# A scan that starts at a constant: where the carried state of a selective scan enters, and who copies it

## The chip, the core and the metric

The kernel runs on one core of a Trainium2 chip. The core has five engines that work at the same time, each through its own queue in the order written: PE (TensorE, matrix products and transposes), DVE (VectorE), ACT (ScalarE), POOL (GpSimd) and SP (SyncE, which here issues nearly all DMAs). An engine that reaches an instruction whose inputs are not there stands still, with all that is queued behind it. The metric is the device time of one execution in microseconds (us), as a median over several runs.

## The reference

The input x is 8 sequences of 2048 rows with 512 channels. The computation is a selective-scan (Mamba) layer followed by a quantised linear layer, both with a residual. Cut to what matters:

```
u     = layernorm(x)
xp    = u @ x_proj_w.T                      # 64 ranks, 16 B, 16 C per row
delta = softplus(xp[:64] @ dt_proj_w.T + b) # per row and channel
for each state n of 16, each channel d, along the rows t:
    h[t] = exp(delta[t,d] * A[d,n]) * h[t-1] + delta[t,d] * B[t,n] * u[t,d]     (h before the first row is 0)
    y[t,d] += h[t] * C[t,n]
x = x + y + u * D
z = layernorm(x);  q = round(z / scale) as int8, scale = max|z| / 127 per row
out = x + (q @ wq.T) * scale * w_scale + bias
```

## The kernel before

The rows are cut into 32 chunks of T = 512 rows; four chunks make one sequence (`CPB` = 4). Channels lie on the 128 partitions in ND = 4 blocks d. Within a chunk the 16 states n follow each other, and within a state the four blocks, which gives `SLOTS` = 64 slots per chunk. The main loop (L972 to L1004) goes through all slots u, with s = u // 4 the running number of the state and d = u % 4. For each slot it emits, in this order: `c_mult` of the state before and every second state a `load_c` (at d = 0), some exponentials, a piece of B for two states later, the matmuls `b_pe` for slot u + 2, the scan of slot u, the transposes `y_pe` for a state some 11 slots back, and whatever the table of planned steps has for this slot. All engines receive their instructions in this order; nothing is reordered later.

What each part does:

- `exp_unit` (L706): ACT computes da = exp(delta * A) for one state and block, 128x512. It runs ahead of the scans by a lead that the tuples `EXP_NONE` (no exponential in this slot) and `EXP_TWO` (two) shape; the lead starts at 7. Ten buffers of 128x512 hold the results.
- `bt_piece` (L715) and `b_pe` (L733): the input term delta*B*u. For ten of the states ACT scales a tile by B (L728) and PE transposes it (L751); for the six `DIAG_STATES` a diagonal matrix comes by DMA (L723) and PE multiplies with it (L742). The result stays in one of three PSUM buffers.
- `scan` (L754): DVE runs the recurrence over 512 rows of one block with one instruction. Its initial value is `0.0 if k % CPB == 0 else state[n][:, d : d + 1]`: a constant in the first chunk of a sequence, and in the other three a column per partition, the state carried from the chunk before. Below, these are called constant chunks (8 of them) and state chunks (24).
- `c_mult` (L779): POOL first copies the last column of h, four numbers per partition, into `state[n]` (L785, not in the last chunk of a sequence), and then multiplies h, 128x2048, with C (L788). h and its product hc have three buffers each.
- `load_c` (L770): SP loads two states' C rows at a time, broadcast over the partitions, into one of three buffers.
- `y_pe`: PE transposes hc and sums it up in PSUM.

Around this, the layer norm, projections and softplus of the next chunk (`prep`) and the residual, quantisation and output of the previous chunk (`post`) are spread over the slots by the tables `PREP_AT` and `POST_AT`; a number is the slot in the chunk that the entry is planned against, and `LATE_AT` takes the place of `POST_AT` near the end. Steps named below: `aggregate` (DVE, L240) finishes the row statistics; `rstd` (POOL, L246 to L252) makes 1/sqrt of them, four small instructions; `norm` of `post` (ACT, L589) applies it; `amax` (DVE, L608) takes the row maxima; `scales` (POOL, L615) writes xs from them; `inverses` (DVE, L620) takes its reciprocal; `dt_pe` (PE, L344) and `softplus` (ACT, L354) make delta through a single PSUM buffer, so that they alternate; `add_bias` (POOL, L601) and `add_x1` (POOL, L669) add 128x1024 tiles. In one slot the steps of `post` stand ahead of those of `prep`.

Of the kernel before, what the change touches and what calls it, by code (L numbers as in the profile page):

```python
# [9 lines left out]
F32 = mybir.dt.float32  # L10
# [17 lines left out]


PREP_AT = dict(  # L30
    stats=(-54, -53, -52, -50),
    aggregate=(-50, -48, -46, -45),
    rstd=-37,
    norm=(6, 6, 7, 10),
    xnt_pe=(10, 12, 13, 15),
    xnt_act=(12, 13, 15, 17),
    xp_pe=(17, 18, 21, 21),
    xp_act=24,
    bt_pe=26,
    bt_act=26,  # L40
    dt_pe=(27, 30, 31, 32),
    softplus=(27, 30, 32, 34),
    dlt_pe=(36, 38, 40, 42),
    du=(37, 39, 41, 43),
)

POST_AT = dict(
    load=(-10, 3),
    residual=(10, 13, 14, 14),
    stats=(15, 17, 19, 23),  # L50
    aggregate=(19, 22, 22, 24),
    rstd=27,
    norm=(29, 29, 29, 34),
    amax=(31, 36),
    scales=37,
    inverses=41,
    add_bias=(30, 38),
    rnd=(47, 47, 49, 49),
    q_pe=(48, 53, 59, 65),
    q_act=(51, 55, 60, 66),  # L60
    o_pe=(57, 62, 68, 71),
    o_out=(59, 64, 70, 73),
    add_x1=(65, 75),
    store=(75, 79),
    add_x=(-1, 0, 8, 10),
)
# [21 lines left out]

Y_BEHIND = 11

LAST_LOAD = (30, 56)
LAST_ADD_X = (50, 52, 61, 62)
SKIP_AT = (44, 46, 55, 57)
EXP_NONE = (6, 8, 9, 11, 12, 16, 18, 20, 28, 29, 30, 31, 32, 33, 34, 37, 45, 50, 51, 54, 56, 62)
EXP_TWO = (0, 1, 3, 4, 10, 15, 19, 22, 23, 24, 35, 36, 39, 41, 42, 43, 46, 53, 57, 58, 61, 63)


@with_exitstack
def kernel(
# [20 lines left out]
    ND = DM // P  # L120
# [4 lines left out]
    CPB = L // T  # L125
# [6 lines left out]
    const = ctx.enter_context(tc.tile_pool(name="const", bufs=1))  # L132
    xpool = ctx.enter_context(tc.tile_pool(name="xp", bufs=3))
    chan = ctx.enter_context(tc.tile_pool(name="chan", bufs=2))
    bcp = ctx.enter_context(tc.tile_pool(name="bc", bufs=3))
    work = ctx.enter_context(tc.tile_pool(name="work", bufs=2))
    small = ctx.enter_context(tc.tile_pool(name="small", bufs=6))
    dram = ctx.enter_context(tc.tile_pool(name="dram", bufs=2, space=bass.MemoryType.DRAM))
    diagd = ctx.enter_context(tc.tile_pool(name="diagd", bufs=1, space=bass.MemoryType.DRAM))
    ps_y = ctx.enter_context(tc.tile_pool(name="ps_y", bufs=1, space=bass.MemoryType.PSUM))  # L140
# [3 lines left out]
    pin = tc.keep_in_program_order  # L144
# [19 lines left out]
    alog_sb = const.tile([P, ND, N], F32, name="alog_sb")  # L164
# [21 lines left out]
    pin(nc.vector.memset(zeros, 0.0))  # L186


    a_exp = const.tile([P, ND, N], F32, name="a_exp")
    pin(nc.scalar.activation(a_exp, alog_sb, AF.Exp))  # L190
    a_neg = const.tile([P, ND, N], F32, name="a_neg")
    diag_d = const.tile([P, ND, P], F32, name="diag_d")
# [80 lines left out]
    def prep(k):  # L273
# [120 lines left out]
    def prep_first(second):  # L394
# [113 lines left out]
        bc = dram.tile([N, T], F32, tag="bc", name="bc_0")  # L508
# [9 lines left out]
        )  # L518
        dt(2)
        dt(3)  # L520
        load_c(0)
        for s in range(2):
            bts[s] = work.tile([P, NT, P], F32, tag="dg", bufs=2, name=f"dg_0_{s}")
            for i in range(NT):
# [5 lines left out]
        for d in range(ND):  # L530
# [8 lines left out]
            t = x[:, :, ts(d, P)]  # L539
# [164 lines left out]
    LAST = NCHUNK * N  # L704

    def exp_unit(u):  # L706
        s, d = divmod(u, ND)
        if s >= LAST:
            return
        k, n = divmod(s, N)  # L710
        t = work.tile([P, T], F32, tag="da", bufs=10, name=f"da_{k}_{n}_{d}")
        pin(nc.scalar.activation(t, delta[k][:, d, :], AF.Exp, scale=a_neg[:, d, n : n + 1]))  # L712
        das[u] = t

    def bt_piece(s, i):  # L715

# [37 lines left out]
    def scan(u):  # L754
        s, d = divmod(u, ND)
        k, n = divmod(s, N)
        if d == 0:
            hs[s] = work.tile([P, ND, T], F32, tag="h", bufs=3, name=f"h_{k}_{n}")
        pin(
            nc.vector.tensor_tensor_scan(  # L760
                hs[s][:, d, :],
                das.pop(u),
                pbs.pop(u),
                0.0 if k % CPB == 0 else state[n][:, d : d + 1],
                ALU.mult,
                ALU.add,
            )
        )

    def load_c(s):  # L770

        if s >= LAST:
            return
        k, n = divmod(s, N)
        t = bcp.tile([P, 2, T], F32, tag="c", name=f"c_{k}_{n}")
        pin(nc.sync.dma_start(out=t, in_=bcs[k][ds(n, 2), :].partition_broadcast(P)))
        cts[s // 2] = t

    def c_mult(s):  # L779
        if s < 0 or s >= LAST - 1:  # L780
            return
        k, n = divmod(s, N)
        h = hs.pop(s)
        if k % CPB != CPB - 1:
            pin(nc.gpsimd.tensor_copy(state[n], h[:, :, T - 1]))  # L785
        hc = work.tile([P, ND, T], F32, tag="hc", bufs=3, name=f"hc_{k}_{n}")
        c = cts[s // 2][:, n % 2, :]
        pin(nc.gpsimd.tensor_tensor(hc, h, c.unsqueeze(1).to_broadcast([P, ND, T]), ALU.mult))  # L788
        hcs[s] = hc
# [51 lines left out]
    def finish():  # L841


        k, s = NCHUNK - 1, LAST - 1
        h = hs.pop(s)
        hc = work.tile([P, ND, T], F32, tag="hc", bufs=3, name=f"hc_{k}_{N - 1}")
        c = cts[s // 2][:, (N - 1) % 2, :]
# [115 lines left out]
    ahead = 7  # L963
    for u in range(ahead):
        exp_unit(u)
    for k in range(NCHUNK):
        plan(k * SLOTS, [(SKIP_AT[i], lambda k=k, i=i: skip_pe(k, i)) for i in range(NT)])
        if k < NCHUNK - 1:
            plan((k + 1) * SLOTS, post(k))
        if k + 1 < NCHUNK:  # L970
            plan(k * SLOTS, [at for at in prep_of[k + 1] if at[0] >= 0 or k > 0])
    for u in range(NCHUNK * SLOTS + Y_BEHIND):  # L972
        k, slot = divmod(u, SLOTS)
        s, d = divmod(u, ND)
# [79 lines left out]
```

## Time and profile before

| what | us |
|---|---|
| median of 3 runs | 2894.75 |
| the runs | 2892.88 to 2896.7 |
| the profiled execution, its own time | 2885.92 |
| its span, first to last instruction | 2884.0 |

| engine | busy us | share |
|---|---|---|
| DVE | 2805.6 | 97% |
| PE | 2766.2 | 96% |
| POOL | 2759.9 | 96% |
| ACT | 2691.9 | 93% |

How to read it: "busy" counts the time in which at least one instruction of the engine was under way. Successive instructions of an engine overlap by some tens of nanoseconds, so the cost of one in a dense row is the distance between two starts, which is less than its duration. The ends of matmuls are modelled, so PE can show as busy while it could take more. A row of instruction groups gives the line, the engine, the operation, out<-in with shapes and the count, then busy time and the mean duration in ns, then the idle time ahead of these instructions and what ended it. A row of the timeline gives start and duration in us, then the same, and in brackets a wait. The granted TensorE clock was 0.992 of full speed over the execution.

### The profile page before, as it was taken

What the parts mean: (1) busy time and instruction counts of PE and PEld (TensorE: products, weight loads), DVE (VectorE), ACT (ScalarE), POOL (GpSimd) and SP (SyncE); (2) the same over time, 40 slices, a digit from 0 to 9 for tenths busy, and PEclk for the clock granted to TensorE, in tenths of its full rate; (3) what the DMA queues carried; (4) which work ended last, traced back from release to release, by engine and by line L of the source; (5) the groups of instructions that cost most, each with busy time, mean ns of one, the idle gap of its engine ahead of it and who ended that gap; (6) DMA issues with size and microseconds to landing.
All of it is one profiled execution on the core that took longest, in us unless ns stands there. A gap on an engine that the chain in (4) does not pass through costs nothing.

```text
span 2884.0 us, 79269 instructions
## 1 busy us (share of the span) xinstructions
PE 2766.2 (96%) x32978; PEld 2350.9 (82%) x32978; DVE 2805.6 (97%) x2949; ACT 2691.9 (93%) x4350; POOL 2759.9 (96%) x1219
## 2 busy tenths in 40 slices
PE   8999999999999999999999999999999999999997
PEld 7888888888888888888888888888888888888875
DVE  6999999999999999999999999999999999999996
ACT  7999999999999999999999999999999999999985
POOL 6899999999999999999999999999999999999997
PEclk9999999999999999999999999999999999999998
DMA  4333333433333333333333333334333333433331
GB/s 149 107 94 89 110 106 111 108 93 97 108 102 117 95 91 106 110 111 104 97 93 111 101 118 96 91 101 115 111 104 95 95 112 100 118 86 101 87 112 51
DMA packets 223655, 295.80 MB, mean 103 GB/s; under 512 B 114048, under 2 KB 114560, under 8 KB 223296
## 3 DMA queue, kind: packets, MB, share of 16 engines
q1 hardware_dynamic: 222240, 290.51, 34.9%
q8 instruction: 258, 4.23, 0.6%
q14 instruction: 101, 0.83, 0.1%
q10 hardware_dynamic: 1056, 0.23, 0.0%
HBM read 252.55 MB, written 38.14 MB: 101 GB/s over the span
## 4 chain that ended last, share of the span: by engine, by line
PE 56%; DVE 26%; issue 8%; ACT 8%; DMA 2%; SPq 0%; POOL 0%; DVEq 0%; ACTq 0%
DVE h L760 20%; PE pb L751 13%; PE pb L742 13%; PE y L810 13%; ACT da L712 3%; PE pdt L344 3%; PE y L831 3%; PE pxp L305 3%; PE po L648 3%; ACT bT L728 2%; PE y L556 2%; PE pz L631 2%; DVE st L236 2%; DVE x L367 2%; DVE am L608 1%
## 5 line engine op out<-in xcount | busy, mean ns | idle before, releaser
L788 POOL TENSOR_TENSOR hc<-h,c 128x2048 f32<-128x2048 f32 x511 | 2327.3, 4560 | 25.4 <-DVE h L760 11.2
L760 DVE TENSOR_TENSOR_SCAN h<-da,state,pb 128x512 f32<-128x512 f32 x1536 | 1859.2, 1260 | 19.2 <-PE pb L742 13.7
L712 ACT ACTIVATE da<-delta,a_neg 128x512 f32<-128x512 f32 x2048 | 1382.6, 714 | 43.4 <-DVE h L760 38.4
L728 ACT ACTIVATE bT<-x,BT 128x512 f32<-128x512 f32 x1276 | 893.7, 713 | 0.0
L742 PE MATMUL pb<-dg,x 128*128 128x128 f32 x6176 | 811.2, 280 | 14.1 <-DMA dg<-dg 8.7
L742 PEld LDWEIGHTS pb<-dg,x 128*128 128x128 f32 x6176 | 746.6, 192 | 76.2 <-DVE h L760 37.7
L751 PE MATMUL pb<-ident,bT 128*128 128x128 f32 x5104 | 731.9, 277 | 47.2 <-DVE h L760 22.0
L751 PEld LDWEIGHTS pb<-ident,bT 128*128 128x128 f32 x5104 | 576.6, 141 | 205.9 <-DVE h L760 77.9
L760 DVE TENSOR_TENSOR_SCAN h<-da,pb 128x512 f32<-128x512 f32 x512 | 591.0, 1200 | 26.6 <-PE pb L742 8.3
L810 PE MATMUL y<-ident,hc 64*128 64x64 f32 x16384 | 613.2, 225 | 0.2
L810 PEld LDWEIGHTS y<-ident,hc 64*128 64x128 f32 x16384 | 547.5, 139 | 73.4 <-issue 48.4
L236 DVE BATCH_NORM_STATS2 st<-x 128x6 f32<-128x512 f32 x244 | 162.9, 668 | 0.0
L669 POOL TENSOR_TENSOR z<-z,x 128x1024 f32<-128x1024 f32 x62 | 149.6, 2412 | 0.0
L601 POOL TENSOR_TENSOR x<-x,bias_b 128x1024 f32<-128x1024 f32 x62 | 146.8, 2368 | 2.5
L344 PE MATMUL pdt<-xp,dtproj_sb 128*128 128x512 f32 x248 | 136.4, 632 | 10.6 <-ACT delta L354 10.2
L354 ACT ACTIVATE delta<-pdt,dtb_sb 128x512 f32<-128x512 f32 x124 | 84.8, 684 | 65.9 <-PE pdt L344 63.2
L831 PEld LDWEIGHTS y<-diag_d,xnT 64*128 64x128 f32 x2048 | 124.6, 187 | 24.1 <-issue 24.1
L831 PE MATMUL y<-diag_d,xnT 64*128 64x64 f32 x2048 | 140.4, 276 | 0.0
L556 PE MATMUL y<-x,ident 128*128 128x256 f32 x512 | 134.6, 386 | 0.0
L648 PE MATMUL po<-wq_sb,qT 128*128 128x512 bf16 x496 | 127.6, 380 | 0.3
L305 PE MATMUL pxp<-xnT,xproj_sb 128*96 128x512 f32 x248 | 124.0, 602 | 3.4 <-ACT xnT L299 3.4
L785 POOL COPY state<-h 128x4 f32<-128x4 f32 x384 | 74.2, 193 | 51.1 <-DVE h L760 36.7
(108 smaller groups left out, 1724.4 us busy)
## 6 DMA issues: line engine op xcount, KB each, us to landing
c<-bc SPq DMA_DIRECT2D x256, 512.0 KB, 4.3
dg<-dg SPq DMA_DIRECT2D x191, 256.0 KB, 5.1
x<-in_x_dram SPq DMA_DIRECT2D x64, 512.0 KB, 4.8
x<-in_x_dram SPq DMA_DIRECT2D x31, 1024.0 KB, 7.2
out_dram<-z SPq DMA_DIRECT2D x62, 512.0 KB, 5.9
dg<-zeros SPq DMA_DIRECT2D x12, 256.0 KB, 6.0
dg<-BT SPq DMA_DIRECT2D x192, 2.0 KB, 4.0
x<-in_x_dram SPq DMA_DIRECT2D x4, 256.0 KB, 4.0
```

The costliest lines, as they stand in the source:

```text
L236: pin(nc.vector.bn_stats(st, src))
L305: nc.tensor.matmul(st["pp"][:E], lhsT=xproj_sb[:, d, :], rhs=xn_t[k][:, d, :], start=(d == 0), stop=(d == ND - 1),)
L344: nc.tensor.matmul(pd, lhsT=dtproj_sb[:, ts(d, P)], rhs=xp, start=True, stop=True)
L648: nc.tensor.matmul(po, lhsT=qt[:, d, :], rhs=wq_sb[:, d, :], start=(d == 0), stop=(d == ND - 1))
L712: pin(nc.scalar.activation(t, delta[k][:, d, :], AF.Exp, scale=a_neg[:, d, n : n + 1]))
L728: nc.scalar.activation(bts[s][:, i, :], xn[k][:, i, :], AF.Copy, scale=b_t[k][:, i, n : n + 1])
L742: nc.tensor.matmul(pb[:, ts(i, P)], lhsT=xn[k][:, i, ts(d, P)], rhs=bts[s][:, i, :], start=True, stop=True,)
L751: pin(nc.tensor.transpose(pb[:, ts(i, P)], bts[s][:, i, ts(d, P)], ident))
L760: nc.vector.tensor_tensor_scan(hs[s][:, d, :], das.pop(u), pbs.pop(u), 0.0 if k % CPB == 0 else state[n][:, d : d + 1], ALU.mult, ALU.add,)
L788: pin(nc.gpsimd.tensor_tensor(hc, h, c.unsqueeze(1).to_broadcast([P, ND, T]), ALU.mult))
L810: nc.tensor.matmul(ys[k, i // 2][:, half, i % 2, d, :], lhsT=hc[rows, d, ts(i, P)], rhs=ident[rows, rows], is_transpose=True, start=first, ...
L831: nc.tensor.matmul(ys[k, i // 2][:, half, i % 2, d, :], lhsT=xn_t[k][rows, d, ts(i, P)], rhs=diag_d[rows, d, rows], start=False, stop=Fals ...
```

## The change

Every scan now begins at a constant: 0.0 in constant chunks, 1.0 in the others. The carried state enters through the first column of da instead: in a state chunk the column holds exp(delta*A) of the first row times the old state. For that:

- `carry_mul` (POOL, once per chunk ahead of a state chunk, slot 36) multiplies A with the first column of delta for all 16 states and four blocks, 128x64, and `carry_exp` (ACT, slot 44) takes the exponential.
- `carry(s + 2)` (POOL, once per state, at d = 0 ahead of `c_mult`) allocates da for a whole state, 128x4x512 with three buffers, and in state chunks writes its four first columns as first_a times `state[n]`.
- `exp_unit` writes columns 1 to 511 only in state chunks, and may not go beyond the state s + 2.
- `keep_state` (ACT, at d = 2 of the next state) copies the last column of h in place of POOL.
- `load_c` loads one state at a time, at d = 2 for the state s + 3, into one of five buffers of half the size.
- Most entries of `PREP_AT` and `POST_AT` and the tuples for exponentials and the skip term have new slots, `small` has five buffers instead of six, and a_exp shares its tile with its input.

```diff
 PREP_AT = dict(
-    stats=(-54, -53, -52, -50),
-    aggregate=(-50, -48, -46, -45),
+    stats=(-53, -53, -50, -48),
+    aggregate=(-49, -49, -44, -39),
-    norm=(6, 6, 7, 10),
-    xnt_pe=(10, 12, 13, 15),
-    xnt_act=(12, 13, 15, 17),
-    xp_pe=(17, 18, 21, 21),
-    xp_act=24,
+    norm=(3, 4, 7, 7),
+    xnt_pe=(9, 11, 14, 15),
+    xnt_act=(11, 13, 15, 17),
+    xp_pe=(17, 17, 21, 24),
+    xp_act=25,
...
-    softplus=(27, 30, 32, 34),
-    dlt_pe=(36, 38, 40, 42),
-    du=(37, 39, 41, 43),
+    softplus=(27, 31, 32, 34),
+    carry_mul=36,
+    carry_exp=44,
+    dlt_pe=(35, 37, 39, 41),
+    du=(37, 38, 41, 43),
 POST_AT = dict(
...
-    aggregate=(19, 22, 22, 24),
+    aggregate=(20, 23, 27, 27),
     rstd=27,
-    norm=(29, 29, 29, 34),
-    amax=(31, 36),
-    scales=37,
-    inverses=41,
-    add_bias=(30, 38),
+    norm=(29, 29, 32, 34),
+    amax=(33, 35),
+    scales=38,
+    inverses=39,
+    add_bias=(30, 45),
...
-    q_pe=(48, 53, 59, 65),
-    q_act=(51, 55, 60, 66),
+    q_pe=(49, 53, 59, 63),
+    q_act=(51, 54, 60, 64),
...
+        def carry_mul():
+            first_a[k] = small.tile([P, N, ND], F32, tag="first_a", bufs=2, name=f"first_a_{k}")
+            pin(
+                nc.gpsimd.tensor_tensor(
+                    first_a[k],
+                    a_neg.rearrange("p d n -> p n d"),
+                    delta[k][:, :, 0].unsqueeze(1).to_broadcast([P, N, ND]),
+                    ALU.mult,
+                )
+            )
+        def carry_exp():
+            pin(nc.scalar.activation(first_a[k], first_a[k], AF.Exp))
...
-        t = work.tile([P, T], F32, tag="da", bufs=10, name=f"da_{k}_{n}_{d}")
-        pin(nc.scalar.activation(t, delta[k][:, d, :], AF.Exp, scale=a_neg[:, d, n : n + 1]))
-        das[u] = t
+        own = slice(0 if k % CPB == 0 else 1, T)
+        pin(
+            nc.scalar.activation(
+                das[s][:, d, own], delta[k][:, d, own], AF.Exp, scale=a_neg[:, d, n : n + 1]
+            )
+        )
+    def carry(s):
...
+        das[s] = work.tile([P, ND, T], F32, tag="da", bufs=3, name=f"da_{k}_{n}")
+        if k % CPB != 0:
+            pin(
+                nc.gpsimd.tensor_tensor(das[s][:, :, 0], first_a[k][:, n, :], state[n], ALU.mult)
+            )
...
-                0.0 if k % CPB == 0 else state[n][:, d : d + 1],
+                0.0 if k % CPB == 0 else 1.0,
...
-        t = bcp.tile([P, 2, T], F32, tag="c", name=f"c_{k}_{n}")
-        pin(nc.sync.dma_start(out=t, in_=bcs[k][ds(n, 2), :].partition_broadcast(P)))
+        t = bcp.tile([P, T], F32, tag="c", name=f"c_{k}_{n}")
+        pin(nc.sync.dma_start(out=t, in_=bcs[k][n, :].partition_broadcast(P)))
...
+    def keep_state(s):
...
         if k % CPB != CPB - 1:
-            pin(nc.gpsimd.tensor_copy(state[n], h[:, :, T - 1]))
+            pin(nc.scalar.copy(state[n], h[:, :, T - 1]))
...
+        if d == KEEP:
+            keep_state(s - 1)
         if d == 0:
+            carry(s + 2)
             c_mult(s - 1)
-            if s % 2 == 0:
-                load_c(s + 2)
-        for _ in range(0 if slot in EXP_NONE else 2 if slot in EXP_TWO else 1):
+        if d == 2:
+            load_c(s + 3)
+        want += 0 if slot in EXP_NONE else 2 if slot in EXP_TWO else 1
+        while want and slot not in EXP_NONE and ahead < (s + 3) * ND:
             exp_unit(ahead)
             ahead += 1
+            want -= 1
```

More of the change, by code (lines that the diff above doesn't have):

```diff
@@ L41 @@
     dt_pe=(27, 30, 31, 32),
-    softplus=(27, 30, 32, 34),
-    dlt_pe=(36, 38, 40, 42),
-    du=(37, 39, 41, 43),
+    softplus=(27, 31, 32, 34),
[3 more added lines that the diff above has]
+    du=(37, 38, 41, 43),
 )
 POST_AT = dict(
-    load=(-10, 3),
-    residual=(10, 13, 14, 14),
-    stats=(15, 17, 19, 23),
-    aggregate=(19, 22, 22, 24),
+    load=(-9, 3),
+    residual=(12, 12, 13, 14),
+    stats=(14, 16, 18, 24),
+    aggregate=(20, 23, 27, 27),
     rstd=27,
-    norm=(29, 29, 29, 34),
-    amax=(31, 36),
-    scales=37,
-    inverses=41,
-    add_bias=(30, 38),
-    rnd=(47, 47, 49, 49),
-    q_pe=(48, 53, 59, 65),
-    q_act=(51, 55, 60, 66),
+    norm=(29, 29, 32, 34),
[3 more added lines that the diff above has]
+    add_bias=(30, 45),
+    rnd=(46, 46, 48, 49),
+    q_pe=(49, 53, 59, 63),
+    q_act=(51, 54, 60, 64),
     o_pe=(57, 62, 68, 71),
     o_out=(59, 64, 70, 73),
-    add_x1=(65, 75),
-    store=(75, 79),
-    add_x=(-1, 0, 8, 10),
+    add_x1=(64, 73),
+    store=(73, 78),
+    add_x=(-3, 0, 10, 10),
 )
@@ L87 @@
 )
+KEEP = 2
 Y_BEHIND = 11
@@ L92 @@
 LAST_ADD_X = (50, 52, 61, 62)
-SKIP_AT = (44, 46, 55, 57)
-EXP_NONE = (6, 8, 9, 11, 12, 16, 18, 20, 28, 29, 30, 31, 32, 33, 34, 37, 45, 50, 51, 54, 56, 62)
-EXP_TWO = (0, 1, 3, 4, 10, 15, 19, 22, 23, 24, 35, 36, 39, 41, 42, 43, 46, 53, 57, 58, 61, 63)
+SKIP_AT = (43, 46, 55, 60)
+EXP_NONE = (2, 4, 6, 8, 9, 11, 14, 16, 20, 28, 29, 30, 31, 32, 33, 34, 46, 48, 49, 50, 54, 56)
+EXP_TWO = (0, 1, 3, 5, 7, 17, 18, 22, 23, 25, 35, 38, 41, 47, 51, 53, 55, 57, 59, 61, 62, 63)
 @with_exitstack
@@ L134 @@
     chan = ctx.enter_context(tc.tile_pool(name="chan", bufs=2))
-    bcp = ctx.enter_context(tc.tile_pool(name="bc", bufs=3))
+    bcp = ctx.enter_context(tc.tile_pool(name="bc", bufs=5))
     work = ctx.enter_context(tc.tile_pool(name="work", bufs=2))
-    small = ctx.enter_context(tc.tile_pool(name="small", bufs=6))
+    small = ctx.enter_context(tc.tile_pool(name="small", bufs=5))
     dram = ctx.enter_context(tc.tile_pool(name="dram", bufs=2, space=bass.MemoryType.DRAM))
@@ L186 @@
     pin(nc.vector.memset(zeros, 0.0))
-    a_exp = const.tile([P, ND, N], F32, name="a_exp")
+    a_exp = alog_sb
     pin(nc.scalar.activation(a_exp, alog_sb, AF.Exp))
@@ L197 @@
     state = [const.tile([P, ND], F32, name=f"state_{n}") for n in range(N)]
+    first_a = {}
     DIAG = DIAG_STATES
@@ L382, in prep @@
         once = dict(xp_act=xp_act, bt_pe=bt_pe, bt_act=bt_act)
+        if k % CPB != 0:
+            once["carry_mul"], once["carry_exp"] = carry_mul, carry_exp
         if k in (1, 2):
@@ L520, in prep_first @@
         dt(3)
-        load_c(0)
+        for s in range(3):
+            load_c(s)
         for s in range(2):
@@ L710, in exp_unit @@
         k, n = divmod(s, N)
-        t = work.tile([P, T], F32, tag="da", bufs=10, name=f"da_{k}_{n}_{d}")
-        pin(nc.scalar.activation(t, delta[k][:, d, :], AF.Exp, scale=a_neg[:, d, n : n + 1]))
-        das[u] = t
+        own = slice(0 if k % CPB == 0 else 1, T)
[5 more added lines that the diff above has]
+    def carry(s):
+        if s >= LAST:
+            return
+        k, n = divmod(s, N)
+        das[s] = work.tile([P, ND, T], F32, tag="da", bufs=3, name=f"da_{k}_{n}")
+        if k % CPB != 0:
+            pin(
+                nc.gpsimd.tensor_tensor(das[s][:, :, 0], first_a[k][:, n, :], state[n], ALU.mult)
+            )
     def bt_piece(s, i):
@@ L761, in scan @@
                 hs[s][:, d, :],
-                das.pop(u),
+                das[s][:, d, :],
                 pbs.pop(u),
-                0.0 if k % CPB == 0 else state[n][:, d : d + 1],
+                0.0 if k % CPB == 0 else 1.0,
                 ALU.mult,
@@ L774, in load_c @@
         k, n = divmod(s, N)
-        t = bcp.tile([P, 2, T], F32, tag="c", name=f"c_{k}_{n}")
-        pin(nc.sync.dma_start(out=t, in_=bcs[k][ds(n, 2), :].partition_broadcast(P)))
-        cts[s // 2] = t
+        t = bcp.tile([P, T], F32, tag="c", name=f"c_{k}_{n}")
+        pin(nc.sync.dma_start(out=t, in_=bcs[k][n, :].partition_broadcast(P)))
+        cts[s] = t
     def c_mult(s):
+        if s < 0 or s >= LAST - 1:
+            return
+        k, n = divmod(s, N)
+        h = hs[s]
+        hc = work.tile([P, ND, T], F32, tag="hc", bufs=3, name=f"hc_{k}_{n}")
+        c = cts.pop(s)
+        pin(nc.gpsimd.tensor_tensor(hc, h, c.unsqueeze(1).to_broadcast([P, ND, T]), ALU.mult))
+        hcs[s] = hc
+    def keep_state(s):
         if s < 0 or s >= LAST - 1:
@@ L784, in c_mult @@
         if k % CPB != CPB - 1:
[L785 to L789, printed above, removed]
+            pin(nc.scalar.copy(state[n], h[:, :, T - 1]))
     def y_pe(s):
@@ L846, in finish @@
         hc = work.tile([P, ND, T], F32, tag="hc", bufs=3, name=f"hc_{k}_{N - 1}")
-        c = cts[s // 2][:, (N - 1) % 2, :]
+        c = cts.pop(s)
         for d in range(ND):
@@ L963 @@
     ahead = 7
+    for s in range(2):
+        carry(s)
     for u in range(ahead):
@@ L971 @@
             plan(k * SLOTS, [at for at in prep_of[k + 1] if at[0] >= 0 or k > 0])
+    want = 0
     for u in range(NCHUNK * SLOTS + Y_BEHIND):
```

## The prediction

> **What bounds the kernel.** I read the page first. Four engines stand at 93% to 97%, so the share names no bound.
>
> ```profile
> span 2884.0 us, 79269 instructions
> PE 2766.2 (96%) x32978; PEld 2350.9 (82%) x32978; DVE 2805.6 (97%) x2949; ACT 2691.9 (93%) x4350; POOL 2759.9 (96%) x1219
> ...
> L788 POOL TENSOR_TENSOR hc<-h,c 128x2048 f32<-128x2048 f32 x511 | 2327.3, 4560 | 25.4 <-DVE h L760 11.2
> L760 DVE TENSOR_TENSOR_SCAN h<-da,state,pb 128x512 f32<-128x512 f32 x1536 | 1859.2, 1260 | 19.2 <-PE pb L742 13.7
> ...
> L760 DVE TENSOR_TENSOR_SCAN h<-da,pb 128x512 f32<-128x512 f32 x512 | 591.0, 1200 | 26.6 <-PE pb L742 8.3
> ...
> L785 POOL COPY state<-h 128x4 f32<-128x4 f32 x384 | 74.2, 193 | 51.1 <-DVE h L760 36.7
> ```
>
> A scan with a state column takes 1260 ns and one with a constant 1200 ns: the kernel already contains the thing that the change makes general. Second view, the timeline of DVE: five scans in a row of each kind, and the first scans of a constant chunk, of the three state chunks after it, and of the next sequence.
>
> ```profile
> 425.54 5.66 DVE L760 TENSOR_TENSOR_SCAN h<-da,pb 128x512 f32<-128x512 f32 x5
> ...
> 513.28 5.96 DVE L760 TENSOR_TENSOR_SCAN h<-da,state,pb 128x512 f32<-128x512 f32 x5
> ...
> 732.79 1.19 DVE L760 TENSOR_TENSOR_SCAN h<-da,pb 128x512 f32<-128x512 f32 x1
> ...
> 819.25 1.25 DVE L760 TENSOR_TENSOR_SCAN h<-da,state,pb 128x512 f32<-128x512 f32 x1
> ...
> 1085.54 1.19 DVE L760 TENSOR_TENSOR_SCAN h<-da,pb 128x512 f32<-128x512 f32 x1
> ```
>
> Start to start a constant scan is 1.115 us and a state scan 1.175: 0.06 less in dense rows too. The constant chunk lasts 819.25 - 732.79 = 86.46 us; the three state chunks 266.29, or 88.76 each. 64 x 0.06 = 3.8 us should lie between them; only 2.3 do. Third view, busy time in these stretches (columns: length, PE, PEld, DVE, ACT, POOL, clock, DMA share, GB/s):
>
> ```profile
> 732.80:819.30 86.50, 84.93 (x1026) 72.52 (x1023) 84.67 (x93) 83.22 (x136) 83.89 (x40) 1.00 0.33 97
> ...
> 908.10:996.90 88.80, 85.98 (x1040) 73.11 (x1036) 88.25 (x92) 84.26 (x137) 86.56 (x42) 1.00 0.35 103
> ...
> sum 352.70, PE 342.69 PEld 291.67 DVE 348.94 ACT 336.27 POOL 343.51; mean PE 85.67 PEld 72.92 DVE 87.24 ACT 84.07 POOL 85.88
> ```
>
> In a state chunk DVE has 0.5 us free: it is the bound. In the constant chunk it has 1.8 us free. What binds there stands in the fourth view, the chain of work for that stretch, which from 781.83 on is nearly all ACT:
>
> ```profile
> 781.83 1.28 ACT L712
> ...
> 788.14 1.23 ACT da L712 x2
> 791.21 1.23 ACT da L712 x2
> ...
> 796.73 2.45 ACT da L712 x4
> ```
>
> So the constant chunk shows the next limit, ACT, and the change puts work on ACT. ACT's own waits there were 1.9 us for dt_pe (L354) and 0.5 for a transpose (L299), together 2.4.
>
> **The change, part by part**, per sequence of four chunks, now 352.75 us (1085.54 - 732.79). PE is left alone: pb transposes follow at 0.11 us where it is not held, so its 96% is modelled ends.
>
> *Scans.* 192 state scans x 0.06 = 11.5 us off DVE: 348.9 to 337.4, 84.4 a chunk. In the whole kernel 1536 x 0.06 = 92 us, the ceiling if nothing else bound.
>
> *POOL.* 48 copies go; starts of copy and following multiply are 0.15 apart, so -7.2. 48 multiplies of 128x4 come. Nearest row: L252, a two-input 128x8 of 206 ns against the copy's 193, so 0.15 with overlap, 0.21 without; I take 0.15 (the copy's overlap), +7.2. Three carry_mul of 128x64: rows of 2412 ns at 1024 and 4560 at 2048 elements give 2.1 ns an element, 0.32 us each. The Trainium skill (GPSIMD Engine Reference, Performance pitfalls for Q7 kernels) speaks against them: reads with a step over 8 bytes cost 2.9 cycles an element and not 1.9, by estimate 64/1.2 GHz = 0.05 more; A is read so. The copy read h at a far larger step for 193 ns, but of four elements nothing can be told. By the row +1.0 a sequence, by the rule +1.1; I take 0.35 each. POOL: about 344.6, and since chunks differ, 84.8 in the constant chunk, 86.8 in the next two, 86.1 in the last.
>
> *ACT.* 48 copies of 128x4 come, 16 in each chunk but a sequence's last. Row of the trace:
>
> ```profile
> 771.69 0.19 ACT L334 COPY BT<-pbt 128x64 f32<-128x64 f32 x1
> 771.78 0.72 ACT L712 ACTIVATE da<-delta,a_neg 128x512 f32<-128x512 f32 x1
> ```
>
> 190 ns long, yet the next starts 0.09 later. This one reads PSUM; the smallest from SBUF (L170, 128x8) lasts 208, less 0.1 of overlap makes 0.11, which I take. The Trainium skill (ScalarE: Activation LUTs, Rules for kernel authors) says to keep simple arithmetic off ScalarE and to budget some 0.3 us an activation; that would be 14.4 us a sequence and the change would lose. By the row it is 5.3. Bounds: 0.09, and 0.21 with no overlap. Each copy waits for the last scan of its state, two slots back; behind it queue exponentials and B pieces, for which PE and DVE wait. ACT sits within three slots of DVE, mostly level with it, so I price this wait at nothing; without that cover it is up to one slot, 1.3 us. carry_exp: the 128x64 exponential L190 takes 256 ns, 0.16 with overlap.
>
> *ACT's waits.* norm(2) moves from slot 29 to 32 and fills 0.7 of the 1.41 us that softplus(2) waited, a copy a little more: -0.8 a chunk. Against it: two aggregates now stand at slot 27, where rstd also stands. POOL reached rstd 0.8 us after scan 27 began, so it waits some 0.6 for them, and norm(0), which began 0.2 us after rstd's end, goes with it: +0.4. ACT per chunk: 84.07 + 16 x 0.11 + 0.16 + 2.4 - 0.8 + 0.4 = 88.0 in three chunks, 86.1 in the last.
>
> *A stall on DVE that the slots bring.* inverses moves from slot 41 to 39, scales from 37 to 38, with carry_mul ahead. Before:
>
> ```profile
> 878.73 0.24 POOL L615 TENSOR_SCALAR xs<-am 128x4 f32<-128x4 f32 x1
> ...
> 880.09 0.15 DVE L620 RECIPROCAL rs<-xs 128x4 f32<-128x4 f32 x1
> ```
>
> xs was ready 1.1 us early. DVE now arrives two scans (2.2) and 16 x 0.06 = 1.0 earlier, POOL 0.35 + 0.6 later: a wait of 3.0 us, with scan 40 and the rest of DVE behind it. DVE's own dense work in a chunk is 64 x 1.113 + 12.4 = 83.7 (starts of L657, L236, L240, L608, L367 added up); with the stall and 1.0 of the waits for pb early in the chunk, 87.7, and 87.3 in the last chunk, which has no carry_mul.
>
> *da.* Release by state instead of by block: the exponential of s + 2 needs all scans of s - 1, which POOL's multiply needs as well; ACT is not far enough ahead for this to bind, nothing. Whether ACT's columns 1 to 511 are ordered behind POOL's column 0 the trace cannot show: nothing if not, and if so ACT waits POOL's lag behind DVE, up to 4 to 5 us in states 7 to 9. I take nothing.
>
> *C and SP.* 256 issues more, 0.32 us each, 2.6 us a chunk on a queue that mostly waits. C landed 4.3 us after an issue that lay at least 17.6 us ahead of its use; the load now stands behind that slot group's diagonal load instead of ahead of it, waits for POOL's multiply of s - 2 and has 14 slots, some 19 us, until its use: hidden. The diagonal of state 9 was issued at least 5.7 us ahead of its scan and lands in 5.1: 0.3 us from one more load ahead of it eats into this, but there DVE waits for ACT anyway. If either came late, POOL or PE would stand for what is missing of 4 to 5 us. *Other slots.* q_pe(3) at 63 now precedes o_out(1) at 64, whose PSUM buffer it takes: PE stands for DVE's 0.73 us, and pb of slot 66 queues behind it, 0.3 us on DVE, which the stall above absorbs because DVE then waits less for xs. The residual copies, transposes and projections move by one to three slots beside ACT and PE work of the same length, between nothing and the 0.5 us of a transpose wait a chunk; I take nothing, as the old order already has two of these waits. Buffers of `small` and the shared a_exp tile: nothing, DVE's order covers them.
>
> **Sum.** Three chunks at 88.0 (ACT), the last at 87.3 (DVE and POOL): 351.3 against 352.75, -1.45 a sequence. Over 31 chunks (7.75 sequences): -11 us. Span 2884.0 to 2873. The median of the runs lies 10.75 above the span, so 2883.5; I say 2883.
>
> **Rivals.**
>
> *The bound is POOL and the waits close up.* For: ACT's 2.4 us are order, not work, and most slots are new. Against: the chain of the constant chunk. Then 86.5 for the constant chunk, 87.0, 87.0, 86.5: 347.0, -5.75 x 7.75 = -45: 2850.
>
> *Nothing to see.* ACT takes back just what DVE gives: with ACT's waits at 2.4 + 0.1 the sum is back at 352.7: 2895.
>
> *Slower: ACT's copies.* Place: keep_state on ACT. Price: 0.21 us each where the overlap is lost, because the copy stands behind a wait. Three chunks become 89.6, sum 356.1, +3.35 x 7.75 = +26: 2921. It decides from 3 x (86.24 + 16c) + 87.3 = 352.75, c = 0.14 us. For: my value is only 0.03 below that. Against: every small ACT row overlaps. The ordering of column 0 would add to this side.
>
> *The change doesn't do what it says:* scans stay at 1260 ns. The constant row with the same operands else speaks against it; I give it no chance of its own.
>
> **Chances.** The runs before spread over 3.8 us, so 0.2%, 5.8 us, is about what can be told. Forecast (-6 to -25) 0.34, POOL-bound 0.20, nothing 0.16, slower 0.30. So faster 0.54, same 0.16, slower 0.30. Range: down to near the POOL-bound case, 2846, up to most of the slower one, 2915; the likeliest case alone is 2870 to 2889.
>
> **What would show it.** All 2048 scans near 1200 ns. ACT copies starting the next instruction 0.11 after them; ACT the busiest engine, above 2740. DVE waiting for xs at L620 in nearly every chunk, some 2 to 3 us. POOL's small multiplies near 200 ns. Wrong if ACT copies cost over 0.14, if the xs wait is absent and chunks fall to 86.5, or if exponentials wait for POOL.

## The result: slower by 0.4%

| | before | after |
|---|---|---|
| median of 5 runs, us | 2896.22 | 2905.97 |
| the runs, us | 2892.88 to 2898.32 | 2904.56 to 2906.61 |
| the profiled execution's span, us | 2884.0 | 2904.4 |
| four chunks in the middle, us | 352.7 | 355.5 |

The ratio of after to before is 1.0036 (95% interval 1.0026 to 1.0047). The forecast was 2883 us and faster; the kernel is slower. The profiled execution of before, 2885.92 us, was some 7 us faster than the fastest of the five runs; that is why the spans and the four chunks differ by more than the medians do.

First the page of the kernel after: its span, the engines' shares, and the groups that the change touches.

```profile
span 2904.4 us, 80256 instructions
PE 2753.6 (95%) x32978; PEld 2354.3 (81%) x32978; DVE 2734.7 (94%) x2949; ACT 2732.1 (94%) x4758; POOL 2772.9 (95%) x1243
...
L798 DVE TENSOR_TENSOR_SCAN h<-da,pb 128x512 f32<-128x512 f32 x2048 | 2362.5, 1202 | 82.5 <-PE pb L780 49.7
L824 POOL TENSOR_TENSOR hc<-h,c 128x2048 f32<-128x2048 f32 x511 | 2329.5, 4564 | 36.2 <-DVE h L798 15.4
...
L750 POOL TENSOR_TENSOR da<-first_a,state 128x4 f32<-128x4 f32 x384 | 83.6, 218 | 34.6 <-DVE h L798 18.9
```

All 2048 scans now take 1202 ns, and DVE is busy for 71 us less than before (2734.7 against 2805.6). No engine stands above 95%, and all but ACT have more free time than before (ACT 172 us against 192). So something waits for something. The smaller groups, by line with shapes kept apart, hold the copies that ACT took over, the `carry_mul` of POOL, and the reciprocal of `inverses`:

```profile
L833 ACT COPY state<-h 128x4 f32<-128x4 f32 x384 | 73.4, 191 | 11.7 <-DVE h L798 11.2
L378 POOL TENSOR_TENSOR first_a<-a_neg,delta 128x64 f32<-128x64 f32 x24 | 10.1, 420 | 0.0
L643 DVE RECIPROCAL rs<-xs 128x4 f32<-128x4 f32 x31 | 5.5, 177 | 52.3 <-POOL xs L638 52.3
```

The last row shows where DVE stands: 31 reciprocals, together 5.5 us of work, with 52.3 us of idle time ahead of them. The waits of DVE, PE, ACT and POOL (us in total, times, longest us):

```profile
DVE rs L643 <- POOL xs L638: 52.3, 30, 2.7
DVE h L798 <- PE pb L780: 49.7, 102, 7.7
DVE h L798 <- PE pb L789: 23.1, 67, 0.9
...
PE pb L780 <- DMA dg<-dg: 33.6, 27, 6.1
ACT qT L660 <- PE pz L654: 41.4, 39, 1.8
POOL ve L252 <- DVE mv L246: 14.6, 30, 0.7
```

Before, DVE waited for xs once, 0.3 us, and for the two kinds of pb:

```profile
DVE h L760 <- PE pb L742: 22.0, 46, 0.9
DVE h L760 <- PE pb L751: 6.0, 19, 0.9
```

52.0 us more for xs and 72.8 - 28.0 = 44.8 more for pb make 97, about as much as the quicker scans could give at the most (92). By stretch, four chunks in the middle (columns: length, PE, PEld, DVE, ACT, POOL, clock, DMA share, GB/s):

```profile
826.50:915.50 89.00, 85.25 (x1030) 73.00 (x1029) 84.95 (x92) 85.81 (x154) 86.59 (x43) 1.00 0.37 103
915.50:1004.50 89.00, 85.27 (x1030) 73.00 (x1028) 85.11 (x92) 85.81 (x154) 87.06 (x43) 1.00 0.39 102
1004.50:1093.20 88.70, 85.25 (x1030) 72.97 (x1028) 84.96 (x93) 84.36 (x139) 86.70 (x40) 1.00 0.41 103
1093.20:1182.00 88.80, 85.16 (x1029) 73.00 (x1028) 84.96 (x92) 85.53 (x152) 85.00 (x29) 1.00 0.37 103
sum 355.50, PE 340.93 PEld 291.96 DVE 339.98 ACT 341.50 POOL 345.35; mean PE 85.23 PEld 72.99 DVE 84.99 ACT 85.38 POOL 86.34
```

Before, the constant chunk was shorter than the others by 2.3 us. Now all four last nearly the same, though their work differs by up to 2 us on POOL and 1.5 us on ACT. A length that does not follow the work of any engine suggests a loop: a chain that goes from engine to engine and comes back to itself one chunk later.

The timeline shows its legs. Here are rows of DVE and POOL of the kernel after, from the reciprocal of chunk 9 to that of chunk 10.

```profile
883.03 1.21 DVE L798 TENSOR_TENSOR_SCAN h<-da,pb 128x512 f32<-128x512 f32 x1
885.40 0.42 POOL L378 TENSOR_TENSOR first_a<-a_neg,delta 128x64 f32<-128x64 f32 x1
885.90 0.24 POOL L638 TENSOR_SCALAR xs<-am 128x4 f32<-128x4 f32 x1
886.17 0.18 DVE L643 RECIPROCAL rs<-xs 128x4 f32<-128x4 f32 x1 [1.93 <-POOL xs L638]
886.27 2.33 DVE L798 TENSOR_TENSOR_SCAN h<-da,pb 128x512 f32<-128x512 f32 x2
...
944.35 2.31 DVE L798 TENSOR_TENSOR_SCAN h<-da,pb 128x512 f32<-128x512 f32 x2
945.72 0.20 POOL L750 TENSOR_TENSOR da<-first_a,state 128x4 f32<-128x4 f32 x1 [0.47 <-ACT da L736]
955.52 0.24 POOL L252 TENSOR_SCALAR ve<-mv 128x8 f32<-128x8 f32 x1 [0.42 <-DVE mv L246]
974.36 0.42 POOL L378 TENSOR_TENSOR first_a<-a_neg,delta 128x64 f32<-128x64 f32 x1
974.87 0.24 POOL L638 TENSOR_SCALAR xs<-am 128x4 f32<-128x4 f32 x1
975.14 0.18 DVE L643 RECIPROCAL rs<-xs 128x4 f32<-128x4 f32 x1 [1.84 <-POOL xs L638]
```

*The DVE leg.* After the reciprocal DVE does scans 40 to 63 and then 0 to 19 of the next chunk. Scan 19 is the first of the two that begin at 944.35; it ends at 945.55. POOL stands for it and goes on at 945.72. The bracket names an exponential of ACT, which ends some 30 ns after the scan; but in all 22 state chunks up to chunk 29 POOL starts 169 to 171 ns after the end of scan 19, also in those where that exponential has ended 130 ns before the scan. So the scan is what it waits for. The leg lasts 945.72 - 886.17 = 59.55 us.

*The POOL leg.* POOL then runs without a pause but 0.42 us: five multiplies with C, `rstd`, `add_bias`, `carry_mul`, `scales`. xs releases the next reciprocal at 975.14. That is 975.14 - 945.72 = 29.42 us.

Together 88.97 us, which is the length of the chunk. Neither engine is full; each stands for the other once a round.

### The profile page after: what moved, and what is told of

The parts are those of the page before. It is cut to its first block, busy times and chain, and to the rows that moved or that the text cites. A ratio compares the mean times of both kernels' runs of the same rounds, so it can differ in the third digit from the quotient of the medians.

```text
span 2904.4 us, 80256 instructions
## 1 busy us (share of the span) xinstructions
PE 2753.6 (95%) x32978; PEld 2354.3 (81%) x32978; DVE 2734.7 (94%) x2949; ACT 2732.1 (94%) x4758; POOL 2772.9 (95%) x1243
## 4 chain that ended last, share of the span: by engine, by line
PE 73%; DVE 12%; DMA 6%; ACT 4%; issue 3%; SPq 1%; POOL 1%; DVEq 0%; ACTq 0%; POOLq 0%
PE pb L780 22%; PE y L854 15%; PE pb L789 15%; DVE h L798 9%; DMA dg<-dg 6%; PE po L671 4%; PE y L579 4%; PE y L875 3%; PE pxp L311 3%; PE pdl L368 2%; PE pz L654 2%; PE pxn L299 2%; ACT da L736 2%; DVE x L373 1%; PE pdt L350 1%
## 5 line engine op out<-in xcount | busy, mean ns | idle before, releaser
L798 DVE TENSOR_TENSOR_SCAN h<-da,pb 128x512 f32<-128x512 f32 x2048 | 2362.5, 1202 | 82.5 <-PE pb L780 49.7
L736 ACT ACTIVATE da<-delta,a_neg 128x511 f32<-128x511 f32 (+1 forms) x2048 | 1380.6, 715 | 1.0 <-DVE h L798 0.6
L780 PE MATMUL pb<-dg,x 128*128 128x128 f32 x6176 | 792.2, 279 | 60.0 <-DMA dg<-dg 33.6
L242 DVE BATCH_NORM_STATS2 st<-x 128x6 f32<-128x512 f32 x244 | 156.5, 672 | 0.0
L579 PE MATMUL y<-x,ident 128*128 128x256 f32 x512 | 126.6, 380 | 0.0
L750 POOL TENSOR_TENSOR da<-first_a,state 128x4 f32<-128x4 f32 x384 | 83.6, 218 | 34.6 <-DVE h L798 18.9
L660 ACT ACTIVATE qT<-pz 128x512 bf16<-128x512 f32 x124 | 73.0, 588 | 42.7 <-PE pz L654 41.4
```

Of the source, the lines that this page charges most:

```text
L579: nc.tensor.matmul(ys[k, i // 2][:, half, i % 2, :, :], lhsT=ident, rhs=t[:, :, half, :], start=False, stop=False, skip_group_check=True,)
L736: nc.scalar.activation(das[s][:, d, own], delta[k][:, d, own], AF.Exp, scale=a_neg[:, d, n : n + 1])
L780: nc.tensor.matmul(pb[:, ts(i, P)], lhsT=xn[k][:, i, ts(d, P)], rhs=bts[s][:, i, :], start=True, stop=True,)
L798: nc.vector.tensor_tensor_scan(hs[s][:, d, :], das[s][:, d, :], pbs.pop(u), 0.0 if k % CPB == 0 else 1.0, ALU.mult, ALU.add,)
```

## The experiments

Ratios are to the kernel before, run on the same chip, with the 95% interval; that kernel took 2886 to 2894 us on the chips of the experiments, so times of different groups are compared by their ratios. Diffs are against the kernel after unless said otherwise. The first four ask whether the wait for xs sets the time at all, or whether the new work, on ACT above all, would hold the chunk at 89 us without it.

**Scales and inverses back at their old slots.**

```diff
-    scales=38,
-    inverses=39,
+    scales=37,
+    inverses=41,
```

> The changed kernel with two entries of one table put back: scales at slot 37 and inverses at 41. Theory S (new slots stall DVE, and through it POOL): the 1.9 us that DVE waits for xs in each chunk go, and with them at least the 0.65 us that POOL then waits at slot 43; 28 chunks x 0.65 to 1.9 us = 18 to 53 us less than the changed kernel's 2906, so 2853 to 2888. Theory W (the work added to ACT and POOL binds, the stall is slack): no change, 2902 to 2908.

Measured: 2854.14 us, ratio 0.9883 (0.9868 to 0.9898). The waits of DVE in it:

```profile
DVE rs L643 <- POOL xs L638: 12.8, 20, 1.9
```

Two numbers of a table turn +0.4% into -1.2%. The theory that the stall sets the time holds; the rival, that the new work holds the chunk at 89 us, falls, for all of that work is still in this kernel.

**The kernel before with only the new slots.** No scan changes, no copy moves, C is loaded by pairs; only the three tables and the tuples are those of the kernel after, without the two carry steps. The part that decides:

```diff
-    scales=37,
-    inverses=41,
+    scales=38,
+    inverses=39,
...
```

> The kernel before with only the new slots: scans from the state column, POOL copies, C in pairs. Theory S: DVE is still at 88 us a chunk and now waits for xs too, 1.12 - 2.34 - 0.6 = -1.8 us at slot 39: 28 x 1.8 = +50, so 2930 to 2950. Theory W: slots matter little, 2890 to 2902.

Measured: 2939.34 us, ratio 1.0182 (1.0165 to 1.0199), +53 us. The waits of DVE:

```profile
DVE rs L620 <- POOL xs L615: 53.7, 31, 2.3
```

The slots alone bring the whole wait for xs, 1.7 us in each of 31 chunks, and the time grows by as much.

**The kernel before with only the constant.** Every scan of the kernel before begins at a constant; the carried state goes nowhere.

```diff
-                0.0 if k % CPB == 0 else state[n][:, d : d + 1],
+                0.0 if k % CPB == 0 else 1.0,
```

> The kernel before with every scan begun at a constant and nothing else; it leaves the carried state out of the scans of 24 chunks. If DVE alone bound the state chunks: 24 x (88.75 - 86.46) = 55 us less, about 2841. If ACT, which was the chain of the constant chunk and lost 1.3 us of its lead there, binds when such chunks follow each other: half of that, 2862 to 2872.

Measured: 2846.13 us, ratio 0.9858 (0.9843 to 0.9872), some -40 us, between the two forecasts. Its waits of DVE for pb are 41.6 and 16.7 us, against 22.0 and 6.0 before, with nothing else edited: a DVE that is quicker stands more for PE. Some of what the scans give is taken back this way, and it belongs to the constant itself, not to the slots.

**The mechanism with the old slots.** All of `PREP_AT`, `POST_AT`, `SKIP_AT`, `EXP_NONE` and `EXP_TWO` as before, the carry steps kept at 36 and 44.

```diff
-    norm=(29, 29, 32, 34),
-    amax=(33, 35),
-    scales=38,
-    inverses=39,
+    norm=(29, 29, 29, 34),
+    amax=(31, 36),
+    scales=37,
+    inverses=41,
...
```

> The changed kernel with the slots of the kernel before for all prep and post steps, the skip term and the exponentials; carry_mul and carry_exp stay at 36 and 44. Theory S (the new slots cost the gain): xs is ready about when DVE asks for it, so a gain over the kernel before shows, 2860 to 2885. Theory W (the work moved to ACT and POOL binds): about like the changed kernel, 2900 to 2915, because the work is the same.

Measured: 2875.95 us, ratio 0.9961 (0.9946 to 0.9976). xs is waited for once, 2.2 us. But the waits of DVE have a new row:

```profile
DVE h L798 <- ACT da L736: 38.2, 54, 1.2
```

The exponentials come late, most of it at slot 36, right behind the slots 28 to 34 that have none. Two things at least are new for them, the copies on ACT and the da tiles of a whole state, which limit their lead; which of the two makes them late was not taken apart. With `scales` and `inverses` at 37 and 41 the other new slots give 0.9883 in place of 0.9961: they pay as a whole, and only these two are badly placed.

The next four test the loop by its length. If the loop is right, each scan that moves from its DVE leg to ahead of the reciprocal takes a scan's 1.11 us off each chunk, and a step taken out of its POOL leg takes its own duration off.

**Inverses one slot later (40).**

> The changed kernel with inverses at slot 40 in place of 39. Theory L (a loop: POOL must reach xs, DVE must go on to the scans that POOL's next multiplies need; the slot decides how many scans stand in the loop's DVE leg): one scan of 1.11 us leaves the leg, so 28 x 1.1 = 31 us less than the changed kernel, a ratio to before of about 0.993; DVE still waits some 0.8 us for xs. Theory P (the old slots 37 and 41 fit for another reason, such as what ACT or PE do at 41): less than 10 us gained, ratio above 1.000.

Measured: 2871.83 us, ratio 0.9924 (0.9912 to 0.9937), and the waits of DVE:

```profile
DVE rs L643 <- POOL xs L638: 29.9, 29, 1.6
```

Against the kernel after, -1.12%, 32 us or 1.0 us a chunk: about one scan.

**Inverses four slots later (43).**

```diff
-    inverses=39,
+    inverses=43,
```

> The changed kernel with inverses at slot 43. Theory L: the wait for xs is gone altogether, and the time is that of slot 41 or up to 8 us less, ratio 0.985 to 0.989. Rival: the rounding on ACT at slot 46 needs the reciprocal and now waits for it, which puts back part: ratio 0.990 or more.

Measured: 2855.33 us (2854.56 to 2858.87), ratio 0.9865 (0.985 to 0.9881). The wait for xs is gone: in the chunk that was looked at xs is written at 957.44 and read at 959.54. Four chunks of this kernel, columns as above:

```profile
723.80:810.60 86.80, 84.86 (x1030) 72.93 (x1029) 84.99 (x93) 84.71 (x152) 85.92 (x29) 1.00 0.41 107
...
984.40:1071.60 87.20, 84.81 (x1029) 72.91 (x1028) 84.70 (x93) 84.23 (x139) 86.72 (x40) 1.00 0.38 105
sum 347.80, PE 339.72 PEld 291.52 DVE 339.34 ACT 339.72 POOL 345.42; mean PE 84.93 PEld 72.88 DVE 84.83 ACT 84.93 POOL 86.35
```

The work of each engine is that of the kernel after, to about 0.5%; the four chunks are 7.7 us shorter. Four scans later does not bring four times 1.11, because after some 2 us the loop is no longer what binds. POOL, busy for 86.35 of 86.95 us a chunk, is the next candidate. By its ratio this is the quickest full version of the study, though the intervals do not part it from the one with inverses at 41; both beat the kernels before and after.

**A shorter POOL leg: the aggregates as before.** Inverses stay at 39. With the last two aggregates at 22 and 24, POOL does not wait for them ahead of `rstd`.

```diff
-    aggregate=(20, 23, 27, 27),
+    aggregate=(20, 22, 22, 24),
```

> The changed kernel with the four aggregates of post back at 20, 22, 22, 24, ahead of rstd at 27; inverses stay at 39. Theory L: POOL's wait of 0.42 us at slot 28 stands in the POOL leg of the loop, so 28 x 0.42 = 12 us less than the changed kernel, ratio to before about 0.9995. Rival: such a small wait is hidden by POOL's later one, no change, ratio about 1.0036.

Measured: 2894.78 us, ratio 0.9999 (0.9991 to 1.0007).

**A shorter POOL leg: carry_mul behind scales.**

```diff
-    carry_mul=36,
-    carry_exp=44,
+    carry_mul=40,
+    carry_exp=50,
```

> The changed kernel with carry_mul at slot 40 and carry_exp at 50, so that POOL writes xs 0.5 us earlier with the same work in all. Theory L: 24 x 0.5 = 12 us less than the changed kernel, ratio about 0.9995. Theory W (POOL's amount of work, not its order, decides): no change, ratio about 1.0036.

Measured: 2895.24 us, ratio 1.0005 (0.9997 to 1.0013). Against the kernel after, the first gives 0.37%, 11 us over 31 chunks or 0.35 each, where the trace shows a wait of 0.42. The second gives 0.31%, 9 us over the 24 chunks with a `carry_mul`, 0.37 each, where the trace shows 0.50. Both steps lie in the loop, and each gives most of its length, or all of it within the intervals. In the second the wait for xs is not shorter (56.3 us in 31 times against 52.3 in 30): DVE loses less between scan 19 and the reciprocal and waits longer at it. The two together, measured as in the table below, fall from 2.94 us a chunk to 2.64, and to 2.55 with the aggregates as before.

The last four start from what binds next, POOL's work.

**The last-column copies back on POOL, behind the multiply; inverses at 43.** The diff is against the version with inverses at 43.

```diff
-            pin(nc.scalar.copy(state[n], h[:, :, T - 1]))
+            pin(nc.gpsimd.tensor_copy(state[n], h[:, :, T - 1]))
...
-        if d == KEEP:
-            keep_state(s - 1)
         if d == 0:
             carry(s + 2)
             c_mult(s - 1)
+            keep_state(s - 1)
```

> The changed kernel with inverses at 43 (ratio to before 0.9865) and the last-column copies back on POOL, behind the multiply of the same state. POOL had no wait left in a chunk there. If POOL's work now sets the time: 48 copies x 0.15 us = 7.2 us more a sequence of four chunks, 55 us in all, ratio about 1.005. If ACT sets it, 48 x 0.09 = 4.2 us less a sequence: ratio about 0.976.

Measured: 2895.01 us, ratio 1.0029 (1.0018 to 1.0041). POOL's share rises to 98%, and its group of copies reads:

```profile
L833 POOL COPY state<-h 128x4 f32<-128x4 f32 x384 | 76.6, 200 | 0.0
```

ACT has less to do here than with inverses at 43 and POOL more, and the time rises: once the loop is open POOL binds, not ACT. The copies' move to ACT is worth the difference of the two ratios (each from its own chip), 1.6% or 47 us: 384 copies at 0.12 us each. The carry multiplies take from POOL what the copies gave.

**All the slots that still had a wait, together; inverses at 43.**

```diff
-    xp_pe=(17, 17, 21, 24),
-    xp_act=25,
+    xp_pe=(17, 18, 21, 21),
+    xp_act=24,
...
-    carry_mul=36,
-    carry_exp=44,
+    carry_mul=40,
+    carry_exp=50,
...
-    aggregate=(20, 23, 27, 27),
+    aggregate=(20, 22, 22, 24),
```

> The changed kernel with inverses at 43, the aggregates at 20, 22, 22, 24, carry_mul at 40 and carry_exp at 50, and the projection steps xp_pe and xp_act at their old slots, which lets the diagonals come about a slot earlier. If POOL's work sets the time, the order of its steps is worth nothing any more once the loop through xs is open: ratio 0.985 to 0.988, as with inverses at 43 alone. If small waits still add up (diagonals that PE waits 1.3 us a chunk for, 0.25 us for the statistics): up to 30 us more, 0.976.

Measured: 2861.28 us, ratio 0.9907 (0.9893 to 0.992), a miss: a little slower than with inverses at 43 alone. The diagonals came on time (PE's wait for them fell from 36.7 to 8.9 us), while ACT's wait for the projection of dt rose from 43.5 to 61.6. Diagonals that come on time bring no gain that shows; which of the three edits costs the 0.4% was not taken apart.

**Scales on DVE.** With inverses at 39, one edit takes POOL out of the way between the row maxima and the reciprocal.

```diff
-            pin(nc.gpsimd.tensor_scalar(xs, st["am"], Q_EPS, 1.0 / 127.0, ALU.max, ALU.mult))
+            pin(nc.vector.tensor_scalar(xs, st["am"], Q_EPS, 1.0 / 127.0, ALU.max, ALU.mult))
```

> The changed kernel with all its slots, inverses at 39 too, but scales, 128x4, on DVE in place of POOL, so that DVE makes xs itself. Loop theory: DVE no longer waits, and POOL has 0.32 us less to do a chunk (31 x 0.32 = 10 us): the time of inverses at 43 or 10 us below, ratio 0.983 to 0.987. Rival: the other 1 to 2 us of waits, for the diagonals above all, take the place of the one removed: ratio 0.993 to 1.000.

Measured: 2935.07 us, ratio 1.0163 (1.0149 to 1.0177). Both expectations miss, and by far. The timeline shows DVE and POOL around it:

```profile
974.88 4.56 POOL L824 TENSOR_TENSOR hc<-h,c 128x2048 f32<-128x2048 f32 x1
975.73 3.74 DVE L638 TENSOR_SCALAR xs<-am 128x4 f32<-128x4 f32 x1
979.38 0.68 DVE L373 TENSOR_TENSOR x<-pdl,x 128x512 f32<-128x512 f32 x1
...
981.33 0.20 POOL L750 TENSOR_TENSOR da<-first_a,state 128x4 f32<-128x4 f32 x1 [1.52 <-DVE rs L643]
```

Four numbers per partition take DVE 3.74 us: the instruction begins while POOL multiplies and ends 28 ns after POOL's multiply ends. The group has 31 of them, and none is quick:

```profile
L638 DVE TENSOR_SCALAR xs<-am 128x4 f32<-128x4 f32 x31 | 111.5, 3596 | 0.0
```

POOL's `da` then waits for DVE, which is late by what it was held: 1.5 us here. The granted clock was lower in this run than in the others, 0.982 to 0.986 against 0.990 to 0.995, so part of the 1.6% may be PE's.

**The same, with less on POOL.** In addition the negated mean of `rstd` goes to DVE and the aggregates go back.

```diff
-    aggregate=(20, 23, 27, 27),
+    aggregate=(20, 22, 22, 24),
...
-        pin(nc.gpsimd.tensor_scalar(nm, mv[:, :, 0], -1.0, None, ALU.mult))
+        pin(nc.vector.tensor_scalar(nm, mv[:, :, 0], -1.0, None, ALU.mult))
```

> As before it, scales on DVE, and in addition the negated mean of rstd (128x8) on DVE and the aggregates at 20, 22, 22, 24. If POOL's work sets the time: another 0.34 us a chunk, 10 us, and the 0.4 us that POOL waits for the statistics: ratio 0.975 to 0.983. If ACT is the next bound, no better than scales alone.

Measured: 2913.66 us, ratio 1.0092 (1.0078 to 1.0106). xs on DVE takes 2603 ns in the mean and again ends just after POOL's multiply each time. At the usual clock (0.991 to 0.993) the kernel is again slower than with inverses at 39 and `scales` on POOL. What POOL was spared is small beside the hold.

## Why the prediction was wrong, by its own steps

*Scans: right.* 1202 ns each. 1.11 us start to start.

*ACT's copies: right.* The timeline of ACT in the kernel after:

```profile
880.63 0.18 ACT L833 COPY state<-h 128x4 f32<-128x4 f32 x1
880.72 0.72 ACT L736 ACTIVATE da<-delta,a_neg 128x511 f32<-128x511 f32 x1
```

The next instruction starts 0.09 us after the copy, at the lower bound of 0.09 to 0.21. The 0.3 us that was set against this stands in the Trainium skill (ScalarE: Activation LUTs, Rules for kernel authors) for an activation whose bias is a column per partition, and the copy has no such operand. The slower rival rested on 0.21 and falls with it: the end was slower, but not by this mechanism.

*POOL: nearly right.* Small multiplies 0.15 us start to start, as taken. `carry_mul` lasts 0.42 us and cost 0.50 to the next start, where 0.35 was taken. The two rows that the prediction names, drawn as a line to 64 elements, give 0.40, not 0.32. That leaves little for the reads with a step, which the Trainium skill warns of (GPSIMD Engine Reference, Performance pitfalls for Q7 kernels); no run changed the step. POOL's busy time of four chunks: 345.35 against 344.6.

*ACT: the work right, its place in the sum wrong.* Its busy time with 2 us of order waits was put down as a chunk of 88.0 us. With inverses at 43 the same instructions run in chunks of 86.8 to 87.2: ACT's waits are not fixed; they close up when nothing else holds the chunk.

*The stall at inverses: foreseen, and right in kind.* "A wait of 3.0 us" was worked out from where DVE and POOL arrive, POOL 0.35 + 0.6 later (measured 0.50 + 0.42). In the trace it is 1.76 us a chunk, mean over the 24 chunks 4 to 27. But DVE also stands for 1.18 us between scan 19 and the reciprocal, where PE also waits some 1.1 us for the diagonal of state 9. POOL's leg runs meanwhile, so what DVE loses there only shortens its wait for xs. 1.76 + 1.18 = 2.94 against 3.0.

*The step that failed is "1.0 of the waits for pb early in the chunk", and with it "87.7".* The remaining standing time of DVE, after the reciprocal and before the next chunk's scan 20, is 2.4 us a chunk and not 1.0. It was found by taking, for each DVE instruction, the distance to the next start less the distance of that kind in dense rows (its 15th percentile). The sum then closes:

| DVE per chunk, us, mean of chunks 4 to 27 | before, measured | after, predicted | after, measured |
|---|---|---|---|
| dense work | 86.33 | 83.7 | 83.51 |
| wait for xs, with what is lost ahead of it since scan 19 | 0.38 | 3.0 | 2.94 |
| standing elsewhere | 1.53 | 1.0 | 2.41 |
| sum | 88.24 | 87.7 | 88.86 |

With 2.4 in place of 1.0 the prediction's own sum is 89.1: above its 88.0 for ACT, and slower than before.

The 1.0 fits the state chunks of the kernel before. There DVE stands in this part of the round for 1.2 us in the first two state chunks of a sequence and 1.6 in the third, but for 2.2 in the constant chunks, whose scans are those that every chunk has now. With the constant alone in the kernel before it is 2.5 in all chunks. So a loss of this size comes with the quicker scans alone, and the kernel before already showed it. (That DVE has 0.5 us free in a state chunk is read from busy time; from start to start it loses 1.3 there.)

In the kernel after the loss is spread otherwise. By slot, in its state chunks: the scans of slots 54 and 58 lose 0.65 us together, as in the constant chunks before (0.66); in its state chunks it was 0.23. Slot 6 loses 0.66 (0.58 before). Slots 2 and 3 lose 0.66 and lost nothing before, nor with the constant alone. There `q_pe(3)`, moved from slot 65 to 63, now stands right ahead of the pb of slot 66, slot 2 of the next chunk:

```profile
917.70 0.66 PE L654 MATMUL pz<-ident,z 128*128 128x128 f32 x4
918.19 0.60 PE L789 MATMUL pb<-ident,bT 128*128 128x128 f32 x4
918.90 4.75 DVE L798 TENSOR_TENSOR_SCAN h<-da,pb 128x512 f32<-128x512 f32 x4 [0.38 <-PE pb L789]
```

The prediction saw this place, at 0.3 us, and let it vanish, "which the stall above absorbs". That is wrong in the loop: the stall absorbs what DVE loses between scan 19 and the reciprocal, and nothing of what it loses from the reciprocal to scan 19, where POOL's release moves with it. Slot 66 is in that second part. (PE does not stand for a PSUM buffer there, as the prediction had it; it is busy.) No run moved `q_pe(3)` alone, so its share is read from the traces only.

The size agrees with the whole: 355.2 us a sequence as a typical value against the 351.3 forecast, 3.9 over 7.75 sequences is 30 us; the span is 2904.4 against the 2873 forecast. That the time itself missed by 23 only is luck: the median of before lay 10.75 above its profiled span, and that of after lies 1.6 above its own.

*The diagonal of state 9, "there DVE waits for ACT anyway".* PE does wait for diagonals, 33.6 us in 27 times against 8.7 in 6. The chain of waits of the kernel after has one of these loads, 7.07 us from issue to landing:

```profile
869.20 7.07 DMA dg<-dg
876.41 2.02 PE pb L780 x16
```

The cover was another than was named: the wait for xs behind it, which gets shorter by what is lost here.

*The rivals.* The one bound by POOL, 347.0 us a sequence and 2850 in all, is what this kernel becomes when one number is changed: 347.8 and 2855. "Nothing" was near in size but gave ACT as the cause, which the same run refutes. The time lies inside the stated range, on the slower side, which had a chance of 0.30; but that side was argued from ACT's copies, so this is luck too.

Put together, as ratios: the constant alone is worth -1.4%; the full mechanism with the state carried along and `inverses` at 43 -1.35%; placing `inverses` at 39 costs 1.7 points of that; the remaining new slots bring 0.8 point, and the copies' move to ACT 1.6. The loads of C by single states and the smaller `small` were not tried alone.

## What to carry to other kernels

When one engine waits for a second once a round, and the second waits for the first elsewhere in the round, do not compare the two engines' sums: add up the legs of the loop, from release to release, and price each delay by the leg in which it lies. A delay beside the other engine's leg is free as long as there is a wait left to absorb it, and one in the loop counts in full or nearly so. A consumer that stands early in a queue is put behind a few instructions that do not need it; here two to four scans, for -1.5% to -1.7%.

## What the hardware did that was not expected

A small DVE instruction with a constant operand, from SBUF to SBUF, can be held for as long as POOL's running multiply. With scales on DVE it took 2.0 to 4.1 us, and each of the 31 ends 25 to 32 ns after a POOL instruction ends: 29 after the multiply with C, two after the `carry_mul` behind it. The reciprocal of the same four numbers is not held: in the version with inverses at 43 it takes 0.15 us at 959.54, in the middle of a multiply of POOL that runs from 957.92 to 962.49. This agrees with the Trainium skill (SBUF — State Buffer, Who interferes with whom): DVE and POOL share a pair of ports, `tensor_scalar` is among the DVE operations that can take it, and whoever comes second is blocked for the whole instruction of the other. That the ports are the cause here no run shows. And here the rule and the measurement part, for not every instruction of POOL holds DVE in this way: in the last run, the negated mean on DVE took 144 to 149 ns beside POOL's power instruction of 1.67 us in 30 of 33 cases, but 1955 ns in the one case in which it fell well into a multiply with C, and ended 27 ns after it.

Less of a surprise, as 0.11 was taken, is how cheap ACT is for very small copies: 0.09 us from start to start for 128x4 from SBUF, against 0.15 us for the same copy on POOL before.
